# The first block of attention products moved in front of the scores, in a fused cross-attention and mixture-of-experts kernel

## The chip, the cores and the metric

The kernel runs on one core of one Trainium2 chip. The metric is the device time of one execution in microseconds (us). Before the change it is 883.15 us, the median of 12 runs (881.21 to 884.96).

A core has four compute engines that run side by side: TensorE (PE in the profile, with its weight loads as PEld), VectorE (DVE), ScalarE (ACT) and GpSimd (POOL). SyncE (SP) issues most DMAs. Each engine works through a queue of its own in order and waits at semaphores for the others. Matrix products land in PSUM, which another engine empties.

## The reference

One gated transformer block over x of 4 batches x 1024 tokens x 256 features, with a context of 64 tokens for each batch, all in float32:

```python
x = x + tanh(g_xattn) * attention(layernorm(x), context, context, ...)
x = x + tanh(g_ffn)   * experts(layernorm(x), ...)

def attention(q, k, v, ...):            # 16 heads of 64 features
    qh, kh, vh = (einsum('bld,hdk->hblk', t, w) for t, w in ((q, w_qs), (k, w_ks), (v, w_vs)))
    attn = softmax(einsum('hblk,hbmk->hblm', qh, kh))
    out = einsum('hblm,hbmk->hblk', attn, vh) * qh        # the product with V, times the query
    return heads_side_by_side(out) @ w_proj.T + b_proj

def experts(x, ...):                    # 8 experts of 1024 hidden features, top 2 of 8
    # silu(x @ w1[e]) @ w2[e], weighted by the softmax of the two chosen logits
```

## The kernel before

**Groups and steps.** The 4096 tokens are cut into 8 groups of 512 tokens (`G`; `NG` = 8, two groups to a batch). A group is four tiles of 128 tokens. The main loop (L1250) runs over g = 0 to 8, and inside it over steps t = 0 to 3. Work of neighbouring groups is interleaved: in step t of round g the kernel makes the scores and the softmax of tile t of group g, while it finishes the attention of group g - 1, makes queries for groups ahead, normalises groups ahead, and routes groups behind. Round 8 has no scores; it only finishes group 7. From round 6 on pieces of the expert phase ("slots") are mixed in.

**Heads.** The 16 heads are 8 pairs. Two heads of 64 features fill 128 partitions, so most things are done pair by pair. Four pairs, which are eight heads, make a half.

**What one step issues, by name and line:**

- `probabilities(g, t, qT)` (L420): 8 products of queries with keys into `sc` (L424), a PSUM tile of two banks from the pool `ps2` with two buffers; then on VectorE the maximum (L433) and the subtraction (L435), on ScalarE the exponential (L438), on VectorE the sum (L440) and its reciprocal (L441), on GpSimd the multiplication that gives `pr` (L443).
- `transpose_probabilities` (L448): 8 transposes of the *previous* step's `pr` into two one-bank tiles `pa` (L454), which ScalarE copies to `aT` (L455).
- `attend(g - 1, pairs, ...)` (L459): the products with V. For each two pairs it takes two one-bank tiles `po`, fills them with four 64-row products (L469, in two parts of 64 partitions each), and VectorE multiplies each `po` by the query and writes the result over it in `qT` (L478). Four pairs are one block: 8 products, four banks, four L478. It needs `aT` of all four tiles of group g - 1.
- `queries(h, ...)` (L404): the query projection of a group ahead, a pair at a time into a one-bank tile `pq` (L408), copied by ScalarE (L416). In step 1 it makes two pairs in rounds 2 to 6, one pair in round 1 and none in round 7.
- `finish(g - 1, t)` (L1183): nothing in step 0, the *second* block of `attend` in step 1, and `project` (L480, products `pp`, L486, added to x by L493) in steps 2 and 3.
- `ln_norm` (L298) transposes normalised rows (`pt_a` for the attention of groups ahead, `pt_b` for the routing of groups behind, L317), and `logits` (L503) makes the router's products `pl`.
- `hidden` (L934) makes an expert's first product `ph` (L954) and `combine` (L1034) its second, `py` (L1109).

**What sets the order.** All one-bank tiles (`pq`, `pa`, `po`, `pp`, `pt`, `ph` and others) share one PSUM pool, `ps1`, of four buffers. A product that starts a new tile waits until an older tile of the pool has been emptied. The order on each engine is fixed when the program is built: a planner goes through the instructions as they are written and takes, on each engine, the earliest written one that it holds ready. So the order is mostly the written one, and instructions that are written later fill places where it expects a wait (transposes and scores are mixed in this way in places of the trace). What the planner fixed is not changed at run time.

**The place of the change.** In step 1 of a round the before kernel issues: scores of tile 1, transposes of tile 0, the first block of `attend`, queries, the second block of `attend` (in `finish`). In step 0 the queries of four pairs come last before it. `placing` (routing positions of groups behind) stands between the old and the new position in the text, but is called only in step 0 of a round, and the first block only in step 1.

Of the kernel before, what the change touches and what calls it, by code (L numbers as in the profile page):

```python
# [21 lines left out]
def kernel(  # L22
# [47 lines left out]
    NP = H // 2  # L70
# [35 lines left out]
    def bank(name, spare=False):  # L106

        if spare:
            return ps2.tile([P, 2, 512], F32, tag="ps2", name=name)[:, 0]
        return ps1.tile([P, 512], F32, tag="ps1", name=name)  # L110
# [138 lines left out]
    def apart(tensor, dma, part=None, behind=()):  # L249

        writers = [writer for name in behind for writer in written[name]]
        tc.declare_no_dep(dma.ins, group=tensor, keep=writers, reason="different rows")
        tc.add_to_no_dep_group(tensor, dma.ins)
        for writer in writers:
            tc.add_manual_dep(
                dma.ins,
                writer.name,
                mybir.DependencyInfo(mybir.DependencyClass.Sync, mybir.DependencyReason.DATA),
                reason="rows of the part",
            )  # L260
        if part:
            written.setdefault(part, []).append(dma.ins)

    def clear(i, n):

        r = table_rows // P // n
        apart(
            "table",
            nc.sync.dma_start(
                table.rearrange("(i p r) w -> i p r w", p=P, r=r)[i],  # L270
                empty.unsqueeze(1).to_broadcast([P, r, RW]),
            ),
            "cleared",
        )
# [50 lines left out]
    def add_bias(g):  # L325
        nc.gpsimd.tensor_tensor(
            xg[g], xg[g], bias.unsqueeze(1).to_broadcast([P, T, D]), ALU.add
        )
# [68 lines left out]
    def halves(name, share="group"):  # L397

        return [block([P, NP // 2, G], f"{name}_{i}", share) for i in range(2)]

    def of_pair(t, p):
        return t[p // (NP // 2)][:, p % (NP // 2), :]

    def queries(g, qT, pairs):  # L404
        for p in pairs:
            pq = bank(f"pq_{g}_{p}")
            for c in range(NC):
                product = nc.tensor.matmul(  # L408
                    pq,
                    wq[:, c, p * P : (p + 1) * P],  # L410
                    nT[g][:, c, :],
                    start=(c == 0),
                    stop=(c == NC - 1),
                )
                pinned(product, (g, p, c) == (0, 0, 0))
            nc.scalar.copy(of_pair(qT, p), pq)  # L416
# [3 lines left out]
    def probabilities(g, t, qT):  # L420

        sc = ps2.tile([P, NP // 2, 2, 2, M], F32, tag="ps2", name=f"sc_{g}_{t}")
        for p in range(NP):
            nc.tensor.matmul(  # L424
                sc[:, p // 2, :, p % 2, :],
                of_pair(qT, p)[:, t * P : (t + 1) * P],
                kT[g // GB][:, p, :],
                start=True,
                stop=True,
            )  # L430
        scv = sc.rearrange("p q r j m -> p (q r j) m")
        mx = small.tile([P, H], F32, tag="mx", name=f"mx_{g}_{t}")
        nc.vector.tensor_reduce(mx, scv, AX.X, ALU.max)  # L433
        pr = soft.tile([P, H, M], F32, tag="pr", name=f"pr_{g}_{t}")
        nc.vector.tensor_tensor(  # L435
            pr, scv, mx.unsqueeze(2).to_broadcast([P, H, M]), ALU.subtract
        )
        nc.scalar.activation(pr, pr, AF.Exp)  # L438
        sm = small.tile([P, H], F32, tag="sm", name=f"sm_{g}_{t}")
        nc.vector.tensor_reduce(sm, pr, AX.X, ALU.add)  # L440
        inverse = nc.vector.reciprocal(sm, sm)  # L441
        newest[:] = [
            nc.gpsimd.tensor_tensor(pr, pr, sm.unsqueeze(2).to_broadcast([P, H, M]), ALU.mult).ins,  # L443
            inverse.ins,
        ]
        return pr

    def transpose_probabilities(g, t, pr, aT):  # L448
        prv = pr.rearrange("p (i j) m -> p i (j m)", j=2)
        n = 512 // P  # L450
        for p0 in range(0, NP, n):
            pt = bank(f"pa_{g}_{t}_{p0}")
            for i in range(n):
                nc.tensor.transpose(pt[:, i * P : (i + 1) * P], prv[:, p0 + i, :], ident)  # L454
            nc.scalar.copy(  # L455
                aT[p0 // n][:, :, t * P : (t + 1) * P], pt.rearrange("p (i q) -> p i q", i=n)
            )

    def attend(g, pairs, qT, aT):  # L459

        for q in range(pairs[0] // 2, pairs[-1] // 2 + 1):


            po = [bank(f"po_{g}_{2 * q + j}") for j in range(2)]
            for r in range(2):
                for j in range(2):
                    half = slice(j * M, (j + 1) * M)
                    i = q * 2 + r
                    nc.tensor.matmul(  # L469
                        po[j][r * DK : (r + 1) * DK],  # L470
                        vs[half, g // GB, i, :],
                        of_pair(aT, i)[half],
                        start=True,
                        stop=True,
                    )
            for j in range(2):
                own = of_pair(qT, 2 * q + j)
                nc.vector.tensor_tensor(own, po[j], own, ALU.mult)  # L478
# [702 lines left out]
    held = {}  # L1181

    def finish(g, step):  # L1183

        qT, aT = held[g]
        if step == 1:
            attend(g, range(NP // 2, NP), qT, aT)
        elif step >= 2:
            project(g, qT, (step - 2) * 2)

    def leave(g):
        apart("out", nc.scalar.dma_start(of[g], xg[g]), f"out{g // HG}")
# [30 lines left out]
    def placing(g):  # L1223
        nonlocal done, in_use
        second["places"] = place(list(range(g - GB + 1, g + 1)), second["routing"], f"{g}")
        if g == HG - 1:
            of_slots, done = early_table()
            tables.append(of_slots)
        elif g == NG - 1:
            of_slots, in_use = late_table(done)  # L1230
            tables.append(of_slots)
# [18 lines left out]
    for g in range(NG + 1):  # L1250
        attention_ends = g == NG
        if g < NG:
            qT, aT = qTs[g], halves(f"aT_{g}", "hidden" if g % 2 and g + 1 < NG else "group")
            held[g] = (qT, aT)
        for h in parts[g]:
            if h == len(qTs):
                qTs.append(halves(f"qT_{h}"))
        for t in range(T):
            if t == 0 and g >= 2:
                leave(g - 2)  # L1260
            if g < NG:
                pr = probabilities(g, t, qT)
            if last:
                transpose_probabilities(*last)

            b = (g - GB - 1) // GB
            ends, behind = b * GB + GB - 1, (g - GB - 1) % GB * T + t if b >= 0 else -1
            if behind == T:
                placing(ends)
            if g and t == 1:  # L1270
                attend(g - 1, range(NP // 2), *held[g - 1])
            for h, pairs in parts[g].items():
                queries(h, qTs[h], pairs[t])
            if 0 <= g - 1 < NG:
                finish(g - 1, t)
            last = (g, t, pr, aT) if g < NG else None
            if g == 0:
                for _ in range(value_parts[t]):
                    next(pending_values)
            if behind >= 0:  # L1280
                after(ends, behind)
            if g == 0 and t == 1:
                tc.keep_in_program_order(nc.scalar.activation(tg, tg, AF.Tanh))
                tc.keep_in_program_order(
                    nc.gpsimd.tensor_scalar(bias, bias, tg[:, 0:1], None, ALU.mult)
                )
                for h in range(2):
                    add_bias(h)
            if g + 2 < NG:
                if t == 0 and (g + 2) % GB == 0:  # L1290
                    stats = ln_stats(list(range(g + 2, g + 2 + GB)), f"a{g + 2}")
                elif t == 2:
                    ln_norm(g + 2, stats, "a")
                    add_bias(g + 2)
            if g < 2:
                clear(g * T + t, 2 * T)
            for _ in range(pieces[g][t] if g in pieces else 0):
                next(slots)
# [53 lines left out]
```

## Time and profile before

| | |
|---|---|
| median of 12 runs | 883.15 us (881.21 to 884.96) |
| the profiled execution: time | 884.91 us |
| its span, first to last instruction | 883.2 us |
| mean granted TensorE clock | 0.987 |
| TensorE busy (PE / weight loads) | 848.0 us (96%) / 660.6 us (75%) |
| VectorE, ScalarE, GpSimd busy | 463.9 us (53%), 237.8 us (27%), 269.2 us (30%) |
| scores L424 / transposes L454 | 512 and 256 records, 275 and 273 ns median of one |
| products with V L469 | 256 records of 64x512, 589 ns median; four run side by side |
| VectorE's L478 | 64 of 128x512, 680 ns median |
| exponential L438, GpSimd's L443 | 1.06 us and 1.90 us of one |
| products with V in time | first at 77.3 us (round 1), last at 409.1 us (round 8) |
| first expert product | 343.9 us |

Every float32 product shows as two records in the trace, so 8 products are "x16". A timeline row merges neighbouring records of one kind: start, length, engine, line, what is written from what, number, and in brackets the engine's idle time just before it and what ended that. Matmuls are pipelined, so merged rows overlap by a little; the distance from the start of one row to the start of the next is what a row takes. Durations in the prediction are from this one profiled execution.

Step 1 of the rounds stands in the trace at about 75 us (round 1), 117 (2), 161 (3), 211 (4), 256 (5), 307 (6), 347 (7) and 402 us (8).

### The profile page before, as it was taken

The page shows a single profiled execution, that of the slowest core. Times are in us where ns is not written, and L with a number is a line of the kernel's source. Part 1 is how long each engine was busy: PE and PEld are TensorE (multiplying, and loading weights), DVE is VectorE, ACT ScalarE, POOL GpSimd, SP SyncE. Part 2 cuts the span into 40 slices and gives each one's busy share as a digit, 9 for nine tenths or more (in the row PEclk, how much of TensorE's full clock was granted, in tenths as well). Part 3 has the DMA queues.
Part 4 walks back from the last instruction along what each step waited for, and adds up shares of the span by engine and source line. Part 5 has one row for each costly group of instructions (what it writes and reads, how often), then busy time and mean ns, then how long its engine had stood idle before and what let it go on. Part 6 is the DMA issues. An engine that isn't in the chain of part 4 may idle for free. (4 is left out here: it accounts for less than half of the span.)

```text
span 883.2 us, 13243 instructions
## 1 busy us (share of the span) xinstructions
PE 848.0 (96%) x4684; PEld 660.6 (75%) x4684; DVE 463.9 (53%) x1136; ACT 237.8 (27%) x380; POOL 269.2 (30%) x216
## 2 busy tenths in 40 slices
PE   8999999999999999998999699999999999999996
PEld 6555858485767767785888487877778888999995
DVE  5466384679557966862137431353543443546520
ACT  2563252334332324440112011121112211212210
POOL 3042212223721373207124531203222223222232
PEclk9999999999999999999999699999999999999998
DMA  9999999201100055326575568674737639656611
GB/s 200 339 340 340 340 346 340 67 1 60 61 25 1 28 176 157 109 82 188 149 203 147 170 149 230 149 223 97 184 96 175 189 74 227 199 138 172 190 22 37
DMA packets 165032, 141.79 MB, mean 161 GB/s; under 512 B 72685, under 2 KB 159076, under 8 KB 161248
## 3 DMA queue, kind: packets, MB, share of 16 engines
q1 hardware_dynamic: 145456, 118.79, 46.1%
q0 software_dynamic: 12912, 17.11, 10.1%
q10 hardware_dynamic: 6592, 4.98, 1.8%
q8 instruction: 39, 0.64, 0.3%
q14 instruction: 33, 0.27, 0.1%
HBM read 78.73 MB, written 62.46 MB: 160 GB/s over the span
## 5 line engine op out<-in xcount | busy, mean ns | idle before, releaser
L954 PE MATMUL ph<-xT,w 128*128 128x256 f32 (+2 forms) x928 | 242.4, 416 | 7.6 <-issue 7.1
L954 PEld LDWEIGHTS ph<-xT,w 128*128 128x128 f32 x928 | 176.5, 193 | 61.9 <-issue 11.2
L1073 POOL DMA_INDIRECT out_dram<-x,ids x69 | 111.9, 1622 | 307.2 <-DVE x L1010 147.1
L962 ACT ACTIVATE hT<-ph 128x1024 f32<-128x1024 f32 (+3 forms) x84 | 70.0, 846 | 269.1 <-PE ph L954 184.8
L443 POOL TENSOR_TENSOR pr<-pr,sm 128x1024 f32<-128x1024 f32 x32 | 61.4, 1918 | 209.3 <-DVE sm L441 143.9
L408 PE MATMUL pq<-nT_a,wq 128*128 128x512 f32 x256 | 116.0, 596 | 5.7 <-DVE qT L478 3.8
L486 PE MATMUL pp<-wp,qT 128*128 128x256 f32 x512 | 115.9, 383 | 1.7 <-issue 1.7
L486 PEld LDWEIGHTS pp<-wp,qT 128*128 128x128 f32 x512 | 97.7, 192 | 22.1 <-issue 9.2
L1109 PE MATMUL py<-w,hT 128*128 128x256 f32 (+1 forms) x608 | 109.6, 352 | 0.0
L1109 PEld LDWEIGHTS py<-w,hT 128*128 128x128 f32 (+1 forms) x608 | 93.1, 176 | 12.0
L408 PEld LDWEIGHTS pq<-nT_a,wq 128*128 128x128 f32 x256 | 46.3, 190 | 58.0 <-issue 44.2
L606 POOL DMA_INDIRECT table<-x,to_row x64 | 62.5, 976 | 42.7 <-DVE x L595 24.8
L424 PEld LDWEIGHTS sc<-keys,qT 128*128 128x128 f32 x512 | 62.6, 192 | 11.2 <-issue 10.8
L424 PE MATMUL sc<-keys,qT 128*128 128x128 f32 x512 | 67.1, 278 | 0.0
L455 ACT COPY aT<-pa 128x512 f32<-128x512 f32 x64 | 34.5, 591 | 84.0 <-PE pa L454 74.1
L433 DVE TENSOR_REDUCE mx<-sc 128x16 f32<-128x1024 f32 x32 | 39.0, 1217 | 27.8 <-PE sc L424 27.7
L1000 PE MATMUL q<-sw,sh 128*128 128x128 f32 x432 | 51.7, 275 | 0.0
L440 DVE TENSOR_REDUCE sm<-pr 128x16 f32<-128x1024 f32 x32 | 39.0, 1218 | 23.9 <-ACT pr L438 21.5
L1000 PEld LDWEIGHTS q<-sw,sh 128*128 128x128 f32 x432 | 50.2, 192 | 0.8
L478 DVE TENSOR_TENSOR qT<-po,qT 128x512 f32<-128x512 f32 x64 | 40.9, 677 | 13.9 <-PE po L469 7.6
L1088 DVE TENSOR_SCALAR x<-py,ids 128x256 f32<-128x256 f32 (+1 forms) x31 | 14.2, 458 | 63.9 <-PE py L1109 61.0
L416 ACT COPY qT<-pq 128x512 f32<-128x512 f32 x64 | 36.5, 580 | 36.5 <-PE pq L408 35.6
(261 smaller groups left out, 859.1 us busy)
## 6 DMA issues: line engine op xcount, KB each, us to landing
w<-in_L_ffn_w_dram SPq DMA_DIRECT2D x58, 1024.0 KB
table<-empty SPq DMA_DIRECT2D x8, 5016.0 KB
x<-table SPq DMA_DIRECT2D x116, 64.0 KB
out_dram<-x ACTq DMA_DIRECT2D x8, 512.0 KB
x<-in_x_dram SPq DMA_DIRECT2D x7, 512.0 KB
out_dram<-x,ids POOLq DMA_INDIRECT x69
wq<-in_L_xattn_w_qs_dram SPq DMA_DIRECT2D x4, 256.0 KB
wv<-in_L_xattn_w_vs_dram SPq DMA_DIRECT2D x2, 512.0 KB
```

The costliest lines, as they stand in the source:

```text
L408: product = nc.tensor.matmul(pq, wq[:, c, p * P : (p + 1) * P], nT[g][:, c, :], start=(c == 0), stop=(c == NC - 1),)
L424: nc.tensor.matmul(sc[:, p // 2, :, p % 2, :], of_pair(qT, p)[:, t * P : (t + 1) * P], kT[g // GB][:, p, :], start=True, stop=True,)
L433: nc.vector.tensor_reduce(mx, scv, AX.X, ALU.max)
L443: nc.gpsimd.tensor_tensor(pr, pr, sm.unsqueeze(2).to_broadcast([P, H, M]), ALU.mult).ins,
L478: nc.vector.tensor_tensor(own, po[j], own, ALU.mult)
L486: nc.tensor.matmul(pp[:, i, :], of_pair(qT, p)[:, t * P : (t + 1) * P], wp[:, p, :], start=(p == 0), stop=(p == NP - 1),)
L606: nc.gpsimd.indirect_dma_start(out=table.rearrange("r (u w) -> (r u) w", w=2), out_offset=bass.IndirectOffsetOnAxis(ap=to_row[:, k, i : i ...
L954: nc.tensor.matmul(ph[:, i, :], a[:, c, f * P : (f + 1) * P], xT[:, c, :], start=(c == 0), stop=(c == NC - 1),)
L962: nc.scalar.activation(hT[f0 // per_tile][:, f1 : f1 + step, :], ph, AF.Silu)
L1000: nc.tensor.matmul(to, left[:, f, :], right[:, f, :], start=not onto and f == 0, stop=f == NF // 2 - 1, skip_group_check=onto,)
L1073: rows_added = nc.gpsimd.indirect_dma_start(out=outf.rearrange("n (h d) -> (n h) d", d=w)[:rows_of], out_offset=bass.IndirectOffsetOnAxis( ...
L1109: nc.tensor.matmul(py[t][i * m : (i + 1) * m], hT[f // per_tile][:, f % per_tile, t * P : t * P + m], b[:, f, i * w : (i + 1) * w], start= ...
```

## The change

In step 1 the call of `attend` for the first four pairs of the group before is written in front of `probabilities` instead of behind `transpose_probabilities` and `placing`. Nothing else differs.

```diff
         for t in range(T):
             if t == 0 and g >= 2:
                 leave(g - 2)
+            if g and t == 1:
+                attend(g - 1, range(NP // 2), *held[g - 1])
             if g < NG:
                 pr = probabilities(g, t, qT)
             if last:
                 transpose_probabilities(*last)
...
             if behind == T:
                 placing(ends)
-            if g and t == 1:
-                attend(g - 1, range(NP // 2), *held[g - 1])
             for h, pairs in parts[g].items():
                 queries(h, qTs[h], pairs[t])
             if 0 <= g - 1 < NG:
                 finish(g - 1, t)
```

## The prediction

> **What bounds the kernel now.** Engines first. The page's first part:
>
> ```profile
> PE 848.0 (96%) x4684; PEld 660.6 (75%) x4684; DVE 463.9 (53%) x1136; ACT 237.8 (27%) x380; POOL 269.2 (30%) x216
> ```
>
> PE is busy 96% of the span, the next engine 53%. The chain that ended last has two pieces at the very end and explains nothing, so I count PE's idle time. What ends it, between 60 and 400 us, in the table of waits:
>
> ```profile
> PE pq L408 <- DVE qT L478: 3.8, 5, 1.4
> PE pt_b L317 <- DVE qT L478: 2.0, 4, 0.7
> PE pq L408 <- DVE pr L435: 1.6, 1, 1.6
> PE pa L454 <- POOL pr L443: 1.5, 1, 1.5
> ```
>
> The columns are total, number and longest. All four stand around or behind the products with V (po) and VectorE's L478, which empties their banks. Step 1 of round 2 (I write group 2), PE's timeline:
>
> ```profile
> 117.09 1.95 PE L424 MATMUL sc<-keys,qT 128*128 128x128 f32 x16
> 118.88 1.04 PE L454 MATMUL pa<-ident,pr 128*128 128x128 f32 x8
> 119.84 1.95 PE L469 MATMUL po<-aT,vs 64*64 64x512 f32 x16
> 122.76 3.70 PE L408 MATMUL pq<-nT_a,wq 128*128 128x512 f32 x8 [0.96 <-DVE qT L478]
> 126.39 1.95 PE L469 MATMUL po<-aT,vs 64*64 64x512 f32 x16
> 128.26 2.05 PE L424 MATMUL sc<-keys,qT 128*128 128x128 f32 x16
> 130.15 1.04 PE L454 MATMUL pa<-ident,pr 128*128 128x128 f32 x8
> ```
>
> and VectorE's (119.26 to 120.45 is the maximum, L433):
>
> ```profile
> 120.56 1.22 DVE L435 TENSOR_TENSOR pr<-sc,mx 128x1024 f32<-128x1024 f32 x1
> ...
> 122.02 1.28 DVE L478 TENSOR_TENSOR qT<-po,qT 128x512 f32<-128x512 f32 x2
> ```
>
> po fills all four one-bank buffers; the query projection (pq) behind it needs one back. Its bank comes free only after L478, and L478 stands behind the softmax's maximum and subtraction, because the scores were issued before po. Those PE waits are what the change touches.
>
> **What is moved.** In groups 1 to 7 one block of po (16 records, 1.87 us of PE from 126.39 to 128.26) goes in front of the scores (sc) and the transposes (pa) of step 1; with it four L478. Counts and sizes of instructions, DMAs included, are the same. Group 8 has no scores in step 1, so nothing changes there. SP's and POOL's queues are not passed: at step 1 no placing stands between the two positions.
>
> Is its input ready? aT's last quarter is transposed in step 0 and copied by 111.1 us in group 2, six before. Its banks? Four pq end just ahead of it, and ScalarE empties the last one 0.2 us later in 0.59 (117.30 to 117.89), so 0.8 us after po's new start; po's second pair of banks is needed half a block in, at 0.94. I take 0. The upper end: in groups 2 and 4 a table load (1.28) and a square root (0.30) stand beside that copy; should they come first, po waits some 1.4 each, 2.8 together. [...]
>
> **What goes away.** L478 starts 1.06 to 1.14 us after po starts where VectorE is free (126.39 to 127.53), and four take 2.48. So the banks are empty 3.6 us after po starts, while sc (1.89 after a po block) and pa run 0.88 us more on banks one and two; pq needs the third at 4.6. Removed: the five pq waits, 0.49, 0.96, 0.49, 1.39, 0.49 in groups 1 to 5, 3.82; in group 6 1.62. Group 7 has no pq:
>
> ```profile
> 347.36 1.95 PE L424 MATMUL sc<-keys,qT 128*128 128x128 f32 x16
> 350.80 1.09 PE L454 MATMUL pa<-ident,pr 128*128 128x128 f32 x8 [1.49 <-POOL pr L443]
> 351.82 4.15 PE L469 MATMUL po<-aT,vs 64*64 64x512 f32 x26
> 356.84 1.08 PE L469 MATMUL po<-aT,vs 64*64 64x512 f32 x6 [0.87 <-DVE qT L478]
> 357.85 2.50 PE L424 MATMUL sc<-keys,qT 128*128 128x128 f32 x20
> ```
>
> Here the pa wait of 1.49 gets a po block in front of it, and the two blocks, 6.03 us from 351.82 to 357.85, are pulled apart: 2 x 1.87 = 3.74 is work, 2.29 is waiting. Removed 3.78. Together 3.82 + 1.62 + 3.78 = 9.2. The pt_b waits in groups 3 and 5 (2.0) come from the second block, which does not move: I keep them; they may go.
>
> **What is late next.** Scores are issued 1.87 us later against the step's start, so their softmax must be done with less PE work left before pa of step 2 asks for it. The shortest chain is in group 1, step 2, without other VectorE work:
>
> ```profile
> 83.96 2.05 PE L424 MATMUL sc<-keys,qT 128*128 128x128 f32 x16
> ...
> 91.40 1.90 POOL L443 TENSOR_TENSOR pr<-pr,sm 128x1024 f32<-128x1024 f32 x1 [7.13 <-DVE sm L441]
> ```
>
> From 83.96 to 93.30 it takes 9.34. PE's work from sc to the next pa, by group 2's rows: sc 1.89, pa 0.88, two pairs of pq 3.63, po 1.87, sc 1.89 = 10.16. That leaves 0.8. Group 1 has one pair (1.72, 131.03 to 132.75): 8.25, so a new wait of 1.1 (0 if something later is pulled forward, 1.45 with its present chain of 9.70). Group 2's present chain is 11.40 (117.09 to 128.49), over by 1.24, but three of the L478 in it will be gone from it; rows of the normalisation (L312) stay, so I take 0.4 for group 2 and for group 4, which looks alike (0 to 1.24 each). Group 6: 10.67 now, 0.2 (0 to 0.51). Groups 3 and 5 have further transposes before that pa: 0. Together 2.1 (0 to 4.4).
>
> Group 7 also gets two more changes between 64-row and 128-row matmuls: pa to po takes 0.96 (118.88 to 119.84), pa to pq 0.88 (130.15 to 131.03), so 0.09 each, 0.2. [...]
>
> **Sum.** -9.2 + 2.1 + 0.2 = -6.9 us. Ends: -9.2 - 2.0 = -11.2, and -9.2 + 4.4 + 0.2 + 2.8 = -1.8. Does it reach the end? The first expert product (ph, 343.90) has its input at 341.74: 2.16 us of slack against a gain of at most 1.6 in the one group after its routing starts; earlier gains bring the routing forward too. From 510 to 700 PE is busy all the time (169.93 of 170 in 530 to 700). I carry all of it. The profiled execution took 884.91, 1.7 outside its span and 1.76 over the median of 883.15; it would take 878.0. Against the median: 876.3, and 872.0 to 881.4.
>
> **Rivals.**
> *The softmax becomes the wait (slower).* VectorE takes instructions in the order fixed at build. If the four L478 run after the scores are there, not under them, the maximum starts up to 4 x 0.62 = 2.48 us late, and the chain with it. For it: in group 4 statistics hold VectorE until 213.88, past the end of sc. Against it: in groups 1, 3 and 5 VectorE was idle 2.85 to 4.3 us before the maximum. In groups 1, 2, 4 and 6 no margin is left, so each us of delay costs 4. It decides from 6.9 / 4 = 1.7 us; at 2.48 it costs 9.9, net +3.0: 886.2.
> *Given back in the expert phase (no gain, or slower).* The table of stretches, its columns length, busy time of PE, PEld, DVE, ACT, POOL, clock, DMA share, GB/s, has
>
> ```profile
> 488.00:494.00 6.00, 2.32 (x10) 1.58 (x9) 1.61 (x11) 0.00 (x0) 4.72 (x5) 0.83 0.82 264
> 494.00:501.00 7.00, 3.48 (x8) 1.84 (x8) 1.90 (x17) 0.00 (x0) 2.89 (x3) 0.50 0.27 98
> ```
>
> 7.2 us without PE work, no releaser named, at half clock after. Its cause is not shown, so a shift against the DMAs may lengthen it. If it doubles and all the gain is kept: 883.5; half of it more and half the gain: 883.3; half of it more and none: 886.8. For it: DMA share 0.82 there. Against it: loads are issued as PE frees buffers, so they shift along.
> *It does nothing.* Scores need no bank of these four; if the plan holds po not ready when pq ends, it puts sc first again, as transposes and scores are mixed already at 95.35 to 98.07: 883.15.
>
> **Chances.** Forecast 0.56 (faster); slower softmax 0.24; given back 0.15, a third of it no change; nothing 0.05. A measurement of this kernel can tell about 0.2%, 1.8 us, from no change. Faster 0.56, same 0.10, slower 0.34. The range goes from 871.5 (half a us under my lower end) to 887.0, which takes in most of the rivals.
>
> **What would show it.** Right: po x16 ahead of sc at step 1 in seven groups; no wait of pq on L478; L478 four in a row under sc; group 7's step 1 some 3.5 us shorter. A wait of pa on POOL pr of about 1.1 in group 1, under 0.6 in 2, 4 and 6. Wrong: pa waits over 1.7 us in those four (first rival); step 1 shorter but the stretch after 400 us longer (second); order unchanged (third).

## The result and the profile after

The changed kernel takes 896.91 us (median, 894.85 to 898.23); the kernel before, beside it, 883.27. The ratio is 1.015, 95% interval 1.0137 to 1.0163: 13.6 us slower, where 6.9 us faster was forecast and the range ended at 887.0. The profiled execution has a span of 895.7 us against 883.2, at a mean clock of 0.983. Page, part 1:

```profile
PE 854.5 (95%) x4684; PEld 661.3 (74%) x4684; DVE 466.6 (52%) x1136; ACT 236.9 (26%) x380; POOL 268.8 (30%) x216
```

The same 4684 records took TensorE 6.5 us longer (848.0 before), and its idle time grew from 35.2 to 41.2 us. So the loss has two halves of 6.5 and 6.0 us: TensorE's records last longer, by a lower clock and by short waits inside rows, and it idles more. The table of TensorE's waits from 60 to 400 us (total, number, longest) shows most of the second half:

```profile
PE pt_b L317 <- DVE qT L478: 5.6, 4, 2.6
PE po L469 <- ACT hT L962: 2.6, 1, 2.6
PE pt_b L317 <- DVE x L312: 2.4, 2, 1.3
PE po L469 <- ACT qT L416: 1.8, 3, 1.1
PE pa L454 <- POOL pr L443: 1.6, 3, 0.6
...
PE pq L408 <- DVE qT L478: 0.2, 1, 0.2
```

The wait that the change was to remove is gone (pq on L478: 3.8 us before, 0.2 now). So are the 1.6 us of pq on L435. In their place stand waits at pt_b, po and pa of 14.0 us in all, where before had 2.0, 0.9 and 1.5.

**Where it goes, group by group.** As a mark I take the start of the first `pp` (L486) of each round, which stands in step 2, counted from the first `pa` of the kernel. Between two marks lies one step 1. How much later each round ends than in the profiled execution of before, in us:

| | 1 | 2 | 3 | 4 | 5 | 6 | 7 | sum | rest |
|---|---|---|---|---|---|---|---|---|---|
| changed | +0.60 | +0.74 | +2.84 | +1.92 | +2.80 | +0.78 | +6.18 | +15.86 | -2.4 |

No round gained; 3, 5 and 7 carry 11.8 of 15.9. These three are also the rounds in which the clock fell: it was granted at 0.97, 0.97 and 0.90 between their marks (49.97, 49.94 and 51.49 us), 8.5 us of clock in all, where before had 1.00 in every round. (15.9 - 2.4 = 13.5; the spans differ by 12.5, since 1.0 us was saved ahead of the first `pa`, where nothing was changed. Behind the mark of group 7 it is the kernel before that lost more clock, by the mean clocks of the spans some 11.5 us against 6.7; that is more than the 2.4 made good there.)

**Group 2, step 1**, TensorE's timeline, to be held against the one in the prediction:

```profile
116.80 1.95 PE L469 MATMUL po<-aT,vs 64*64 64x512 f32 x16
118.67 2.05 PE L424 MATMUL sc<-keys,qT 128*128 128x128 f32 x16
120.56 1.04 PE L454 MATMUL pa<-ident,pr 128*128 128x128 f32 x8
121.44 3.60 PE L408 MATMUL pq<-nT_a,wq 128*128 128x512 f32 x8
124.97 2.95 PE L469 MATMUL po<-aT,vs 64*64 64x512 f32 x16
127.85 2.05 PE L424 MATMUL sc<-keys,qT 128*128 128x128 f32 x16
130.45 1.09 PE L454 MATMUL pa<-ident,pr 128*128 128x128 f32 x8 [0.55 <-POOL pr L443]
```

The order is the one forecast and pq no longer waits (0.96 before). But the second po block takes 2.95 instead of 1.95, and pa waits 0.55. Why po takes longer stands on ScalarE:

```profile
123.36 0.58 ACT L416 COPY qT<-pq 128x512 f32<-128x512 f32 x1 [1.03 <-PE pq L408]
123.96 1.28 ACT L438 ACT_TABLE_LOAD   x1
125.25 1.06 ACT L438 ACTIVATE pr<-pr 128x1024 f32<-128x1024 f32 x1
126.22 0.57 ACT L416 COPY qT<-pq 128x512 f32<-128x512 f32 x1
```

The second pq was finished at about 125, and the copy that empties its bank begins only at 126.22, behind the table load and the exponential. The second block of po needs that bank. Before, the scores and so the exponential came a block earlier, and pq was held back by its own wait; the two did not meet. Of the 0.96 won, 1.00 goes back here and 0.55 at pa.

**Group 3** loses at the routing transposes pt_b. VectorE before, and after:

```profile
168.79 0.24 DVE L441 RECIPROCAL sm<-sm 128x16 f32<-128x16 f32 x1
168.95 0.63 DVE L478 TENSOR_TENSOR qT<-po,qT 128x512 f32<-128x512 f32 x1
169.50 2.73 DVE L312 TENSOR_SCALAR x<-x,mv_b,rstd_b 128x256 f32<-128x256 f32 x4
172.15 2.47 DVE L478 TENSOR_TENSOR qT<-po,qT 128x512 f32<-128x512 f32 x4
```
```profile
170.74 0.25 DVE L441 RECIPROCAL sm<-sm 128x16 f32<-128x16 f32 x1
170.91 2.95 DVE L312 TENSOR_SCALAR x<-x,mv_b,rstd_b 128x256 f32<-128x256 f32 x4
173.78 2.47 DVE L478 TENSOR_TENSOR qT<-po,qT 128x512 f32<-128x512 f32 x4
```

The kernel binds the four L312 behind the reciprocal of the softmax (L441). The scores came a block later, so the reciprocal came later too (8.90 us behind the start of step 1, 7.39 before), and so did L312, and the L478 of the second block stands behind L312. TensorE needs those banks for pt_b:

```profile
170.01 1.95 PE L469 MATMUL po<-aT,vs 64*64 64x512 f32 x16
174.51 0.33 PE L317 MATMUL pt_b<-ident,x 128*128 128x128 f32 x1 [2.55 <-DVE qT L478]
175.11 1.54 PE L317 MATMUL pt_b<-ident,x 128*128 128x128 f32 x7 [0.27 <-DVE qT L478]
176.44 1.49 PE L424 MATMUL sc<-keys,qT 128*128 128x128 f32 x6
```

The wait was 0.71 + 0.27 before. And the next records are slow: seven transposes in 1.54 (0.98 before), six score records in 1.49 (0.83). The table of stretches, after its length and the five engines' busy times, gives the granted clock, the DMA share and GB/s:

```profile
170.60:174.00 3.40, 1.36 (x16) 0.32 (x8) 3.37 (x7) 0.10 (x1) 1.90 (x1) 1.00 0.00 0
174.00:177.40 3.40, 2.62 (x13) 2.43 (x14) 2.25 (x4) 0.93 (x2) 0.00 (x0) 0.70 0.00 0
177.40:180.80 3.40, 3.40 (x33) 2.47 (x33) 0.60 (x3) 0.15 (x1) 0.00 (x0) 0.79 0.00 0
```

Missing clock of 0.30 and 0.21 over 3.4 us each is 1.7 us: one stretch of 3.4 us at half clock. Group 5 shows the same (2.55 + 0.27, then seven pt_b in 1.75).

**Group 7**:

```profile
356.20 1.09 PE L469 MATMUL po<-aT,vs 64*64 64x512 f32 x8
359.85 2.47 PE L469 MATMUL po<-aT,vs 64*64 64x512 f32 x8 [2.55 <-ACT hT L962]
362.24 2.46 PE L424 MATMUL sc<-keys,qT 128*128 128x128 f32 x16
364.54 1.04 PE L454 MATMUL pa<-ident,pr 128*128 128x128 f32 x8
365.50 1.95 PE L469 MATMUL po<-aT,vs 64*64 64x512 f32 x16
367.38 3.39 PE L424 MATMUL sc<-keys,qT 128*128 128x128 f32 x28
371.94 0.41 PE L317 MATMUL pt_b<-ident,x 128*128 128x128 f32 x2 [1.17 <-DVE x L312]
...
373.83 1.54 PE L317 MATMUL pt_b<-ident,x 128*128 128x128 f32 x6 [1.26 <-DVE x L312]
```

The moved block asks in its second half for banks that hold the expert products ph of step 0; ScalarE empties them (hT, L962) only behind this step's exponential and a table load. Two stretches at half clock follow (3.4 us at 360, 6.8 at 373).

### The profile page after: what moved, and what is told of

It reads as the page before. It is cut to its first block, busy times and chain, and to the rows that moved or that the text cites. A ratio compares the mean times of both kernels' runs of the same rounds, so it can differ in the third digit from the quotient of the medians.

```text
span 895.7 us, 13242 instructions
## 1 busy us (share of the span) xinstructions
PE 854.5 (95%) x4684; PEld 661.3 (74%) x4684; DVE 466.6 (52%) x1136; ACT 236.9 (26%) x380; POOL 268.8 (30%) x216
## 5 line engine op out<-in xcount | busy, mean ns | idle before, releaser
L962 ACT ACTIVATE hT<-ph 128x1024 f32<-128x1024 f32 (+3 forms) x84 | 69.9, 846 | 266.6 <-PE ph L954 182.4
L443 POOL TENSOR_TENSOR pr<-pr,sm 128x1024 f32<-128x1024 f32 x32 | 61.4, 1917 | 220.8 <-DVE sm L441 175.6
L486 PE MATMUL pp<-wp,qT 128*128 128x256 f32 x512 | 114.0, 379 | 2.3 <-issue 2.3
L486 PEld LDWEIGHTS pp<-wp,qT 128*128 128x128 f32 x512 | 97.0, 190 | 21.6 <-issue 8.5
L606 POOL DMA_INDIRECT table<-x,to_row x64 | 62.2, 972 | 42.7 <-DVE x L595 24.8
L424 PEld LDWEIGHTS sc<-keys,qT 128*128 128x128 f32 x512 | 64.0, 197 | 14.7 <-issue 13.5
L424 PE MATMUL sc<-keys,qT 128*128 128x128 f32 x512 | 69.4, 284 | 0.0
L478 DVE TENSOR_TENSOR qT<-po,qT 128x512 f32<-128x512 f32 x64 | 40.3, 674 | 18.7 <-PE po L469 13.0
L469 PE MATMUL po<-aT,vs 64*64 64x512 f32 x256 | 39.0, 621 | 6.4 <-ACT hT L962 2.6
```

Source lines behind the costliest of these rows:

```text
L424: nc.tensor.matmul(sc[:, p // 2, :, p % 2, :], of_pair(qT, p)[:, t * P : (t + 1) * P], kT[g // GB][:, p, :], start=True, stop=True,)
L486: nc.tensor.matmul(pp[:, i, :], of_pair(qT, p)[:, t * P : (t + 1) * P], wp[:, p, :], start=(p == 0), stop=(p == NP - 1),)
L606: nc.gpsimd.indirect_dma_start(out=table.rearrange("r (u w) -> (r u) w", w=2), out_offset=bass.IndirectOffsetOnAxis(ap=to_row[:, k, i : i ...
L962: nc.scalar.activation(hT[f0 // per_tile][:, f1 : f1 + step, :], ph, AF.Silu)
```

## The experiments

Each run's ratio is to the kernel before on the same chip. The first four (e1 to e4) ran on a chip on which that takes 880.3 us, g1 to g3 on one on which it takes 864.6, the others on a third with 864.8 or 864.6; on these two the pause of 7 us without matmuls in 488 to 501 us is missing from the traces (TensorE is busy 10.00 of 10.00 us from 490 to 500 in one of them). Ends of spans are therefore not compared between traces, only the marks of the rounds, which agree to 0.02 us where nothing differs (0.09 in group 6). The table has them, in us later than before:

| run | 1 | 2 | 3 | 4 | 5 | 6 | 7 | sum | ratio (95%) |
|---|---|---|---|---|---|---|---|---|---|
| e1 groups 3, 5 moved | 0.00 | 0.00 | +2.63 | -0.01 | +2.73 | -0.08 | +0.02 | +5.29 | 1.0056 (1.0043-1.0069) |
| e2 group 7 moved | 0.00 | 0.00 | 0.00 | 0.00 | 0.00 | -0.08 | +1.29 | +1.21 | 1.0014 (1.0002-1.0026) |
| e3 groups 1, 2, 4, 6 | +0.60 | +0.74 | 0.00 | +1.78 | 0.00 | +0.66 | +1.52 | +5.30 | 1.0059 (1.0042-1.0076) |
| e4 half a block, all | -0.62 | -0.68 | +0.42 | -0.15 | +0.43 | -0.60 | -0.39 | -1.59 | 0.9981 (0.9967-0.9994) |
| e5 wait filled in 3, 5 | +0.60 | +0.74 | +1.28 | +1.77 | +1.28 | -0.94 | +2.15 | +6.88 | 1.0106 (1.0092-1.0121) |
| e7 L312 released | +0.60 | +0.74 | -1.34 | +1.78 | -1.33 | -0.94 | +3.25 | +2.76 | 1.0048 (1.0036-1.0060) |
| b7 before, L312 released | 0.00 | 0.00 | +0.48 | -0.01 | -0.85 | -0.08 | +6.21 | +5.75 | 1.0070 (1.0058-1.0082) |
| e9 groups 1 to 6 | +0.60 | +0.74 | +1.28 | +1.78 | +2.66 | -0.95 | +3.04 | +9.15 | 1.0119 (1.0104-1.0134) |
| f7 released in 3, 5 | +0.60 | +0.74 | -1.33 | +1.77 | -1.32 | -0.95 | +6.43 | +5.94 | 1.0056 (1.0038-1.0074) |
| f8 the same, ph later | +0.60 | +0.74 | -1.34 | +1.78 | -1.33 | -1.02 | +5.89 | +5.32 | 1.0061 (1.0046-1.0077) |
| c7 half, released 3, 5 | -0.63 | -0.68 | -0.98 | -0.15 | -0.97 | -1.22 | -0.32 | -4.95 | 0.9955 (0.9938-0.9972) |
| e8 changed, ph later | +0.60 | +0.74 | +2.73 | +1.76 | +2.74 | -0.94 | +4.28 | +11.91 | 1.0153 (1.0134-1.0172) |
| g1 f7 without group 6 | +0.61 | +0.74 | -1.34 | +1.80 | -1.33 | -0.16 | +0.83 | +1.15 | 1.0024 (1.0014-1.0033) |
| g2 f7, scatters early | +0.60 | +0.74 | -1.33 | +1.79 | -1.33 | -1.02 | +0.92 | +0.37 | 1.0018 (1.0008-1.0027) |
| g3 c7, scatters early | -0.62 | -0.68 | -0.98 | -0.13 | -0.98 | -1.14 | +0.22 | -4.31 | 0.9948 (0.9935-0.9961) |

### Which groups lose: e1, e2, e3

The condition of the moved call, and of the call left at the old place, was restricted to some groups:

```diff
-            if g and t == 1:
+            if g in (3, 5) and t == 1:          # e2: (7,)   e3: (1, 2, 4, 6)
                 attend(g - 1, range(NP // 2), *held[g - 1])
...
+            if g and g not in (3, 5) and t == 1:
+                attend(g - 1, range(NP // 2), *held[g - 1])
```

> The first block goes in front of the scores in rounds 3 and 5 only. Theory T (losses are local: the softmax of step 1 starts 1.9 us later, VectorE's L312 and the second block's L478 queue behind its reciprocal, PE waits 2.8 us for banks at pt_b instead of 1.0 and then runs at half clock): PE's marks in the two traces give +2.8 us for round 3 and +2.8 us for round 5, so 883.3 + 5.6 = 888.9. Rival R (the loss comes from a displaced whole, plan or DMAs, so that parts do not add up): 883 or near 897. Rival S (each round pays alike for late scores, 14 / 7 = 2.0 each): 887.2, and no half clock.

> The first block goes in front of the scores in round 7 only. T: round 7 alone lost 6.2 us between its scores and the first py (first block waits 2.6 us for the banks of ph, which ScalarE empties only behind an exponential and a table load; half clock; pt_b waits 2.4 us for L312); the later phase gave 2.4 us back, which may or may not belong to it: 887.1 to 889.5. R: 883 or 897. S: 885.3.

> The first block goes in front of the scores in rounds 1, 2, 4 and 6 only. T: marks give +0.6, +0.7, +1.9, +0.8 us, so 883.3 + 4.0 = 887.3, with PE waits at the second block for pq's copies (behind the exponential on ScalarE) and 0.5 us at pa on GpSimd's L443, and no half clock in these rounds. R: 883 or 897. S: 891.3.

Groups 3 and 5 lose 2.6 and 2.7 alone, nearly what they lose in the changed kernel: their loss is local. Groups 1, 2 and 4 repeat theirs to 0.15. Group 7 does not: moved alone it loses 1.3, not 6.2, and in e3, where it was not moved at all, it lost 1.5 (pa waited 3.0 for L443, 1.5 before). So something reaches group 7 from the groups ahead of it.

### Half a block: e4

```diff
-                attend(g - 1, range(NP // 2), *held[g - 1])
+                attend(g - 1, range(NP // 4), *held[g - 1])
...
+            if g and t == 1:
+                attend(g - 1, range(NP // 4, NP // 2), *held[g - 1])
```

> Half of the block (four heads, two L478) goes in front of the scores in all rounds, the other half stays behind the transposes. T with the clock as a threshold: scores are 0.94 us late instead of 1.87, so the pt_b wait in rounds 3 and 5 stays near 1.9 us and most of the half-clock stretches go away: +3 to +5, 886 to 888. If cost simply goes with the size moved: +6.8, 890. R: anything.

Two po banks instead of four stand ahead of the scores, and these come 0.94 us later instead of 1.87. The pq waits go as well, groups 1, 2, 4 and 6 gain, and the wait at pt_b in 3 and 5 is 1.34 + 0.27 with no half clock behind it (seven pt_b in 0.98). The kernel is 0.2% faster than before. I had expected 3 to 5 us more than before, as this wait stayed: that missed. The idea is right in direction; its size is what loses.

### The half clock: e5

The scores of step 2 were computed a second time, ahead of pt_b, in groups 3 and 5; nobody reads the first result. (The rest of the edit only lets `probabilities` write into a given tile.)

```diff
+            if g in (3, 5) and t == 1:
+                early.append(scores(g, 2, qT))      # 16 records, overwritten unread
             if behind >= 0:
                 after(ends, behind)
```

> The changed kernel, in which the sixteen score products of step 2 of groups 3 and 5 are computed once more, ahead of the routing transposes pt_b: some 1.9 us of added TensorE work in each of the two groups, whose result nobody reads, exactly where TensorE waits 2.55 us for L312 and then runs pt_b and the scores at half clock. Theory A (the wait is long enough to bring the clock down, and the half clock costs more than the wait that the work fills): the wait left is under 1 us, no stretch at half clock follows, pt_b x7 takes 1.0 instead of 1.6 us, and the kernel is FASTER than the changed one by about 2 x 1.2 us in spite of 3.7 us of added work: 1.0 to 3.5 us faster. Theory B (pt_b is slow for another reason, the clock plays no part): the added work only fills the wait, the time stays within 0.5 us of the changed kernel, or grows by up to 3.7 us.

TensorE's timeline of group 3 (line numbers are up to 10 higher):

```profile
171.91 2.05 PE L428 MATMUL sc<-keys,qT 128*128 128x128 f32 x16
174.53 0.33 PE L317 MATMUL pt_b<-ident,x 128*128 128x128 f32 x1 [0.57 <-DVE qT L488]
175.13 0.98 PE L317 MATMUL pt_b<-ident,x 128*128 128x128 f32 x7 [0.27 <-DVE qT L488]
175.95 0.83 PE L428 MATMUL sc<-keys,qT 128*128 128x128 f32 x6
```

pt_b begins as late as in the changed kernel, but runs at 0.98 and the scores at 0.83. Adding 3.7 us of work brought groups 3 and 5 from +2.84 and +2.80 to +1.28 each, and, on another chip and with groups 6 and 7 less late as well, the ratio from 1.015 to 1.0106. So of each loss about 1.5 us is clock and 1.3 us is wait. Whether the clock falls also depends on when the wait comes: in e9, with the same wait of 2.55, group 3 kept its clock (1.00 from 172.0 to 182.2, +1.28) and group 5 lost it (0.56 from 273.8 to 277.2, +2.66). Of eight such waits in the changed kernel, e1, e8 and e9, seven were followed by half clock; of the two of 1.34 in e4 none was.

The traces show why. In those of before and of the changed kernel the granted clock is either full or half, and it changes on a grid of 3.413 us (in the changed kernel it is half from 175.38 to 178.80, one stretch, and from 373.36 to 380.18, two), so one can read what TensorE did in the grid stretch just ahead. In the seven cases it worked for 0.6 to 1.5 us of the 3.4 (in e1, e8 and e9 the mean clock of neighbouring 3.4 us places the grid); in e9's group 3 the wait was shared by two stretches with 2.05 and 1.95 us of work; in e4 the waits of 1.34 and 0.27 leave 1.8 or more of any 3.41 us. In the two traces nine stretches at full clock were followed by half clock, and they held 2.09 us of work or less (2.09, 1.46 and 0.26 in before; 0.60, 0.72, 1.00, 1.46, 1.22 and 0 in the changed kernel, the last of each at the kernel's end); the 492 others held 1.53 or more. From 1.53 to 2.09 us both kinds occur, so these traces give no sharp line, only a region near half a stretch.

### What makes pt_b wait: e7, b7, f7

The binding of L312 behind the reciprocal was taken away in all groups (e7; b7 the same in the kernel before), then in groups 3 and 5 alone (f7):

```diff
-            with behind_sums() if name == "b" else nullcontext():
+            with nullcontext():                                                              # e7, b7
+            with behind_sums() if name == "b" and g not in (0, GB) else nullcontext():       # f7
                 scale = nc.vector.tensor_scalar(
```

> The changed kernel, with the routing normalisation (L312) no longer held behind the reciprocal of the softmax sums. Theory A (rounds 3 and 5 lose because the scores are 1.9 us later, the reciprocal with them, and the four L312 that are held behind it): L312 runs earlier under TensorE's work, the wait of pt_b (2.55 us) falls under 1.5, the half clock behind it goes, and groups 3 and 5 lose nothing any more: 3 to 6 us less than the changed kernel, about 9 us above the kernel before. Theory B (what holds pt_b there is the second L478 block, not L312's place): the wait moves to another instruction and the time stays within 1 us of the changed kernel.

> Control for the run before this one: the kernel before, with the same edit to L312 alone. Theory A: pt_b's wait there is 0.72 us and brings no half clock, so that at most 2 x 0.7 us is to be had: 0 to 1.5 us faster than the kernel before. Theory B: no more and no less than the same edit gives in the changed kernel.

> The changed kernel, with L312 released from its place behind the reciprocal in groups 3 and 5 alone (bound as before in group 7). TensorE's order is that of the changed kernel to the instruction; only VectorE's differs, in eight L312. Theory A (groups 3 and 5 lose through L312 and the half clock alone): the projection behind group 5 starts within 1 us of the time of the kernel before, and the end is decided by group 7: between 0 and 5 us above the kernel before, 0.0 to 0.55%. Theory C (group 7 loses because the groups ahead are late): with them on time it loses 1 to 2 us, as where it was moved alone, so 0.0 to 0.25%. If group 7 loses by itself: 6 us, 0.7%.

In f7 the condition takes in groups 3 and 5 (the rows that they normalise are those of groups 0 and `GB` = 2). Group 3 of f7, on VectorE and TensorE:

```profile
172.19 2.48 DVE L478 TENSOR_TENSOR qT<-po,qT 128x512 f32<-128x512 f32 x4 [0.17 <-PE po L469]
172.94 0.33 PE L317 MATMUL pt_b<-ident,x 128*128 128x128 f32 x1
```

With L312 a step earlier, around step 0's subtraction instead of behind step 1's reciprocal, the second block's L478 follow the reciprocal (171.77 to 172.02) at once, and the first pt_b waits for nothing. Groups 3 and 5 go from +2.8 each to -1.3 each, in f7 with TensorE's order unchanged to the instruction. So the change gains there what the prediction hoped for, as soon as nothing that it makes late stands in front of L478. The control b7 gains little in these groups (+0.48 and -0.85).

I expected no loss from b7; it lost 6.2 in group 7, and e7 3.25. VectorE's timeline of b7 says why:

```profile
350.69 1.38 DVE L312 TENSOR_SCALAR x<-x,mv_b,rstd_b 128x256 f32<-128x256 f32 x4 [2.93 <-DMA out_dram<-x]
351.99 1.22 DVE L433 TENSOR_REDUCE mx<-sc 128x16 f32<-128x1024 f32 x1
```

In group 7 the released L312 stands ahead of the next maximum, and by the trace it waits 2.93 us for a store from x; the softmax and all of VectorE's queue wait with it, and TensorE's next scores wait 4.77 us for the subtraction (L435).

### Why group 7 loses: e9, e8, f8, g1, g2

Four ways to take something away: group 7 put back (e9), two of the three ph pieces of step 0 moved to step 1 in the changed kernel and in f7 (e8, f8), group 6 put back in f7 (g1), and all groups moved as in f7 but the scatters into the table issued eight and eight instead of six, six and four (g2):

```diff
-    pieces = {HG + 2: (0, 0, 1, 1), HG + 3: (3, 3, 2, 2), ...        # e8, f8
+    pieces = {HG + 2: (0, 0, 1, 1), HG + 3: (1, 5, 2, 2), ...
```
```diff
-            first, last = min(6 * (step - 4), 2 * R), min(6 * (step - 3), 2 * R)       # g2, g3
+            many = 8 if step < 8 and g == HG - 1 else 6
+            first, last = min(many * (step - 4), 2 * R), min(many * (step - 3), 2 * R)
```

> The changed kernel, with group 7 alone put back (its eight heads' products stand behind the transposes again), groups 1 to 6 moved. Theory A (group 7 loses by its own move: its first block then asks for banks that hold ph, which ScalarE empties late): the start of the last group's projection is about 9.7 us later than before, as after group 6, and the end about 7 us later: 890. Theory C (group 7 loses because the groups ahead of it are late, whatever its own order): that start is 13 to 16 us later, as in the changed kernel, and the time 894 to 897.

> The changed kernel, with two of the three pieces of expert work (ph) of group 7's step 0 put in step 1, nothing else. Theory A (group 7 loses by its own move, through ph's banks): the wait of po for ScalarE's hT (2.55 us) and the half clock behind it go, 3 to 5 us faster than the changed kernel, 1.0 to 1.2% above the kernel before. Theory C (group 7 loses because the groups ahead are late): the wait moves to the next instruction, VectorE's softmax or ph itself, and the time stays within 1 us of the changed kernel, 1.4 to 1.7%.

> As the run before this one, and in group 7 two of the three pieces of expert work (ph) of step 0 are put in step 1, behind the products with V, so that the moved block does not ask for banks that ph has just filled. Theory A: no wait of po on ScalarE's hT in group 7, 0.4 to 1.3 us faster than the run before this one. Theory C: that wait is small where the groups ahead are on time (0.4 us where group 7 was moved alone), so within 0.5 us of the run before this one.

> The changed kernel with L312 released in groups 3 and 5 (5.0 us above the kernel before, of which group 7 loses 6.4), and group 6 alone put back; group 7 stays moved. Theory D (group 7 loses because group 6's move makes the softmax of its step 2 1.9 us later, on GpSimd the scatters into the table (L606) queued behind that softmax, the gather behind them, VectorE's L928 that waits for the gather, and the softmax of group 7 behind L928): in group 7 po waits for hT at most 0.5 us instead of 2.0, no score runs at half clock there, group 7 loses 1 to 2 us, and the kernel is 3 to 5 us faster than with group 6 moved, 0.0 to 0.3% above the kernel before. Theory E (group 7's own move and the others' together, not group 6's): group 7 still loses 5 us or more, 0.5% or more above the kernel before.

> The changed kernel with L312 released in groups 3 and 5, all seven groups moved, and the sixteen scatters into the table (L606) of groups 0 to 3 issued in the first two steps of group 6, eight each, instead of six, six and four: the last four no longer stand behind GpSimd's L443 of step 2. TensorE's order is the same to the instruction. Theory D: the gather comes 2 to 4 us earlier, L928 no longer waits past the scores, po's wait for hT in group 7 (2.0 us) falls under 0.5, and 2 to 4 us are won against the six, six and four, less up to 1 us that L443 behind eight scatters comes late in group 6: 0.1 to 0.4% above the kernel before. Theory E: group 7's waits stay, and the time is the same or up to 1 us more, 0.5 to 0.7%.

e9: not moved, group 7 still loses 3.0. Its mark is 9.15 us late, near the 9.7 that I expected of theory A, but by luck: the groups ahead are 6.1 late, not 9.7. e8: with ph out of the way pa waits 3.58 for L443 instead of po 2.55 for hT; group 7 loses 4.3 instead of 6.2, on another chip, and the ratio is 1.0153. Beside f7, on the same chip, f8 gains 0.5 us in group 7 and nothing in the ratio. So ph's banks are where the loss shows, not its cause. f7 puts the other theory out too: there the groups ahead are 0.5 us *early* (sum over groups 1 to 6: -0.49), and group 7 loses 6.4. So both theories behind these runs fell. What is left stands on the queues of group 6. GpSimd before, then in f7:

```profile
317.72 1.01 POOL L606 DMA_INDIRECT table<-x,to_row  x1 [0.16 <-issue]
...
326.02 1.90 POOL L443 TENSOR_TENSOR pr<-pr,sm 128x1024 f32<-128x1024 f32 x1 [0.96 <-issue]
...
331.92 0.96 POOL L606 DMA_INDIRECT table<-x,to_row  x1 [0.30 <-issue]
```
```profile
320.08 1.01 POOL L606 DMA_INDIRECT table<-x,to_row  x1 [0.16 <-issue]
...
327.44 1.91 POOL L443 TENSOR_TENSOR pr<-pr,sm 128x1024 f32<-128x1024 f32 x1
...
333.36 0.96 POOL L606 DMA_INDIRECT table<-x,to_row  x1 [0.30 <-issue]
```

The scatters of group 6 (L606) are bound behind a softmax and queued on GpSimd behind its L443. The softmax came later in step 1, the scatters with it, and the gather of the next expert's tokens behind the scatters. VectorE transposes those tokens (L928) and stands still until they come, with the statistics and the maximum of group 7's softmax behind it. The row of L928 in before, f7, g1 and g2:

```profile
341.03 0.71 DVE L928 STREAM_TRANSPOSE xT<-x 128x512 f32<-128x512 f32 x1 [3.90 <-DMA x<-table]
```
```profile
342.04 0.71 DVE L928 STREAM_TRANSPOSE xT<-x 128x512 f32<-128x512 f32 x1 [5.34 <-DMA x<-table]
```
```profile
339.38 0.71 DVE L928 STREAM_TRANSPOSE xT<-x 128x512 f32<-128x512 f32 x1 [3.29 <-DMA x<-table]
```
```profile
335.77 0.71 DVE L928 STREAM_TRANSPOSE xT<-x 128x512 f32<-128x512 f32 x1 [2.89 <-DMA x<-table]
```

In before it begins 0.2 us ahead of the scores of group 7's first step (341.25), in f7 1.2 us behind them (340.81), in g1 0.8 ahead (340.21), in g2 4.5 ahead (340.29). In the changed kernel it is 1.9 behind (351.79 to 349.94). In f7 the maximum is late by that much, then the exponential, then the table load, and hT comes 2.00 us after po asks for it; half clock follows (the next sixteen score records take 3.59 us, 2.05 in e2). In g1 and g2 the same wait is

```profile
347.88 1.57 PE L469 MATMUL po<-aT,vs 64*64 64x512 f32 x8 [0.38 <-ACT hT L962]
```
```profile
347.96 1.57 PE L469 MATMUL po<-aT,vs 64*64 64x512 f32 x8 [0.38 <-ACT hT L962]
```

and group 7 loses 0.8 and 0.9. g2 keeps every move of f7 and its order on TensorE; only the place of scatters on GpSimd differs, and it gives 5.6 us (sum +0.37 for +5.94). Both runs came in much as the theory of the scatters (D) expected; it had put the gain of g2 at 2 to 4 us.

Two limits belong to the 5.6. First, it is read from one execution of each, f7's 1.0 us over its median and g2's 0.9 under; the medians, on two chips with the same time before, give 4.7 (870.23 and 865.52), the ratios 3.3. Second, most of it is clock: in f7 the clock is 0.90 over the 51.75 us from mark to mark, 5.1 us, in g1 and g2 it is 1.00 (over the whole spans 0.991, 0.997 and 0.997). e5, which has the late scatters too, has L928 only 0.5 behind the scores and one stretch at half clock (six pt_b in 1.53, 1.09 in f7), and loses 2.15. The late scatters set the wait; what it costs depends on the grid of the clock as well.

What group 7's own move does is the 0.4 us at po and the waits of pt_b on L312 (e2: 2.4 us where before had none, with a stretch at half clock behind them, six pt_b in 1.54), against 1.5 and 0.9 won at pa and po.

### A version that beats both: c7, g3

c7 is e4 with f7's release of L312 in groups 3 and 5; g3 has the early scatters too.

> Half of the change (four of the eight heads in front of the scores, four at the old place) in all seven groups, with L312 released in groups 3 and 5. Theory A: the half alone was 0.2% faster than the kernel before and still waited 1.34 + 0.27 us for pt_b in groups 3 and 5; released, these go: about 2 to 3 us more, 0.4 to 0.6% faster than the kernel before. Theory B (another chain takes the place of L312 there): no more than the half alone, 0.1 to 0.3% faster.

> Half of the change in all seven groups, L312 released in groups 3 and 5 (0.45% faster than the kernel before), and the scatters eight and eight as in the run before this one. Theory D: L928 waited 4.4 us for the gather there, but no TensorE wait hung on it except 0.8 us for GpSimd's L443 in group 7: 0 to 0.8 us more, 0.45 to 0.6% faster than the kernel before. Theory E: no difference to the half with L312 released.

c7 is 0.45% faster than before (860.63 us against 864.62) and every group gains. The scatters add nothing to it (0.9948 against 0.9955, intervals overlapping): in c7 at most the 0.80 us that pa waits for L443 in group 7 could hang on L928, and in g3 pa still waits there, in three places, 1.12 in all.

## Why the prediction was wrong

**What was removed (-9.2): right for groups 1 to 6, wrong for 7.** The five pq waits (3.82, of which 0.16 stays in group 4) and group 6's 1.62 are gone, L478 stands under the scores, and the order is as written. In group 7 the 3.78 did not come out as time: the waits at pa and at L478 went (e2 gained 1.5 and 0.9 by them), but po waited 2.55 for ph's bank instead. The step that took po's bank wait for 0 looked at pq's copy in groups 1 to 6 and not at ph's in group 7.

**po's banks (0, at most 2.8): the wrong block was examined.** The first block waits for nothing in groups 1 to 6, as said. The second one follows pq directly, and in groups 1, 2, 4 and 6 waits for ScalarE's copy of pq behind the exponential: po takes 2.77 and 2.95 in groups 1 and 2 (2.37 and 1.95 before), waits 1.11 in one place of group 4 and 0.70 in two of group 6. From the second block's start to the next scores the four groups take 0.4, 1.0, 2.2 and 2.1 us longer than before, 5.7 together, where the sum had 0 and its upper end 2.8. Removing pq's wait brought pq to meet the exponential that the same change had delayed.

**The pa waits (2.1): about right.** 0.54, 0.55 and 0.55 in groups 1, 2 and 4 (1.1, 0.4 and 0.4 were forecast). The first rival, the softmax becoming the wait, had the right sign, but it priced 2.48 us of this wait in each of four groups; 0.55 came, and in three of them. The changed kernel is slower for other reasons.

**Groups 3 and 5 (the pt_b waits "come from the second block, which does not move: I keep them"): failed.** The block does not move, but its L478 stand on VectorE behind L312, L312 is bound behind the reciprocal, and that moved by 1.5 us against the step, while TensorE came to pt_b 0.65 earlier. The wait grew from 0.7 to 2.55: 1.3 us per group net of the pq wait that went, and 1.5 more for the clock, of which the sum had no term. e1, e5 and f7 show each part.

These terms add up: 5.3 removed, 5.7 at po, 1.6 at pa, 3.7 at pt_b and 3.4 of clock make 9.1 of the 9.7 us by which groups 1 to 6 end late.

**"SP's and POOL's queues are not passed": true of the order, not of the time: the failed step of the group that lost most.** No instruction of theirs changed place, but GpSimd's L443 came later and with it what is queued behind. The sum read the end of L928 (341.74) only for what it leaves ph, not for what stands behind it on VectorE. That costs group 7 5.5 us by the marks of f7 against g1 and g2 (3.3 to 4.7 by their times), in the group where I counted the largest gain. For the changed kernel itself, with L312 bound, it is argued from the same rows (L928 waits 5.96 there) and from e3, where group 6 was moved, 7 not, and 7 lost 1.5; g1 and g2 were not run with L312 bound.

**The expert phase** was no rival in the end: of 15.9 us, 2.4 are made good behind group 7, not lost.

**Open** stay group 6, where the changed kernel's profile has +0.78 and e5 to f8 have -0.95: VectorE idles 1.58 us before L668 in that profile (0.66 in e3, which has +0.66) and not in theirs, on another chip, and the trace names only a product pq that L668 does not read; group 4, where po's second block takes 4.05 us to the next scores instead of 1.88, pa waits 0.55 and pq 0.16 for 1.39 won, which makes 1.5 of the 1.9; and the changes between 64-row and 128-row matmuls, 0.2 us by the forecast from rows of 0.96 and 0.88, too small to be told.

## What to carry to other kernels

When work is put in front of a softmax, follow the softmax's lateness through every engine that has something bound or queued behind it, not only to the next instruction that reads its result: here a normalisation on VectorE, a bank copy on ScalarE and scatters on GpSimd each carried a delay of 1 to 2 us to a place where TensorE had no slack. A wait that is removed often separated two things; look what meets once it is gone. And a wait can have a second price: here, on an engine 96% busy, seven of eight waits of 2.55 us were followed by half clock, and half of the move gained 0.2% where the whole lost 1.5%.

## What the runs showed of the hardware

- A wait of TensorE of 2.55 us, a transpose and 0.27 us more was followed by some 3.4 us at half clock in seven of eight cases, of 1.34 and 0.27 in neither of two; filling it with 1.9 us of useless products made a group 1.5 us faster.
- In the traces of before and of the changed kernel the clock was full or half and changed on a grid of 3.413 us. It was never halved behind a stretch in which TensorE had worked for more than 2.09 us, and always behind one with less than 1.53 (nine stretches with half clock behind them, 492 without).
- Four L312 take 1.38 us where GpSimd is idle (359.19 in before), and 2.95 where its L443 of 1.90 us runs meanwhile (170.91). The difference of 1.57 is near L443's whole length, so that VectorE seems to stand for most of it. That is an estimate from these two rows; no run here isolates the cause.
